# Two bottleneck blocks with batch normalization: normalizing the first group of a slot inside the first convolution, a shorter mean in the last statistics, and idle matmuls in three pauses

## The chip, the cores and the metric

The kernel runs on one core of a Trainium2 chip. Five engines of the core work side by side, each in its own order: TensorE (PE in the profile; PEld is its loading of weights), VectorE (DVE), ScalarE (ACT), GpSimd (POOL) and SyncE (SP), which here only issues transfers. Engines wait for each other by semaphores. The metric is the device time of one execution in microseconds. Before the change the median of three runs is 1983.51 us (1981.97 to 1983.78).

## The reference

The input x has 64 images of 1024 channels and 14 x 14 pixels, in fp32. Two blocks follow each other. Each is:

```python
out = relu(_bn(_conv(x, w1, b1, 1, 0), g1, be1))    # 1x1, 1024 -> 256 channels
out = relu(_bn(_conv(out, w2, b2, 1, 1), g2, be2))  # 3x3, 256 -> 256 channels
out = _bn(_conv(out, w3, b3, 1, 0), g3, be3)        # 1x1, 256 -> 1024 channels
out = softplus(residual_scale)[0] * out
return relu(x + out)
```

`_bn` subtracts the mean over all images and pixels of a channel and multiplies by the inverse root of the variance, so no value of a convolution can be normalized before all of that convolution has been computed. That is where the borders between stages come from.

## The kernel before

**Layout.** Channels lie on the 128 partitions. The 256 middle channels are two *slots* (MS = 2) of 128, and `y_all` holds them for all 12544 pixels. The pixels are cut in 32 tiles of two images (T = 32, 392 pixels), or, for the second convolution, in eight groups (NG) of eight images (1568 pixels).

**First convolution.** `Conv1` computes one unit (a pair of tiles in block 0, one tile in block 1) by seven matrix products `p1` to `p7` in place of eight (a Strassen form, class `Seven`). `stream` runs the units behind each other; the last two products of a unit, `p4` and then `p3`, are issued within the next unit, or at the end for the last one. `p4` gives the result of slot 1, which ACT evicts; `p3` gives a part of slot 0, which DVE evicts with `scalar_tensor_tensor` (L371). After each result `bn_stats` collects its statistics (L374). In block 1 this stage runs together with the last convolution of block 0 (`fused`).

**Second convolution.** `conv2` is a 3x3 convolution in a form with transformed filters (loaded by SP as tiles `ua` and `ub`) and transformed rows. It begins with four matmuls of the identity into the `columns` banks (L553). The first group of pixels has to be normalized first: `first_norm(s)` computes scale and shift of a slot (`affine_of`), then ACT normalizes the lower rows of the group (L529) and DVE the upper six (`norm_vector`, L535 and L537). `combine` then makes the inputs of the products for slot 1 and after it for slot 0: `steps` (L576; two rows are scaled by ACT, L573), `r` (L665), `sums` (L607), `v` (L613) and `diffs` (L623). PE multiplies `sums`, `v` and `diffs` by the filters, into `columns`, `m` and `l`; results come out as `f` (L780, L782). Each later group is normalized by ACT while the one before it is computed.

**Gram.** The statistics of the last convolution are not taken from its output. `gram` normalizes y again with the second convolution's statistics (`norm_to`: L529 on ACT, L974 on DVE), transposes it in pieces `zt` (the first seven by PE, L1004, and copied by DVE, L1010; the others by transfers into the buffers `homes` and DVE's transpose, L1016), and multiplies each piece with itself into the banks `cp` and `ap`.

**Last statistics.** `conv3_stats` makes mean and variance of the 1024 output channels from these: `g0` and `g1` are the sums divided by the number of pixels, with the mean of each slot in their last column (`means`). Six products `t0`, `t1` of g with the weights w3 follow, DVE multiplies them by w3 again (`q`, L1085 and L1086), and one-column matmuls into the bank `ax` sum over partitions: 16 for the mean (8 output slots, 2 input slots each; L1089), 8 for the second moment (L1091). Before them PE computes the first two of eight products of the first tile (`made`, L1353), which stay in PSUM until scale and shift are known. `residual` then finishes the first tile, and `fused` (block 0) or `final` (block 1) the others.

**What sets the order.** A scheduler orders the instructions of each engine by priorities; `tc.keep_in_program_order` holds an instruction to the place where the program issues it. PE's matmuls, many of DVE's and ACT's steps at the borders are held so. Each engine takes its instructions strictly in its order, so one that waits holds back those behind it.

Of the kernel before, what the change touches and what calls it, by code (L numbers as in the profile page):

```python
# [37 lines left out]
FP = mybir.dt.float32  # L38
# [49 lines left out]
def bottlenecks(ctx: ExitStack, tc: tile.TileContext, x, w1s, w2s, w3s, pars, out):  # L88
# [77 lines left out]
    def matmul(*args, **kw):  # L166

        tc.keep_in_program_order(nc.tensor.matmul(*args, **kw))  # L168

    def filters(pieces, spare):  # L170


# [149 lines left out]
    class Conv1(Seven):  # L322
# [2 lines left out]

        prefix = "a"

        def __init__(self, psum, pool, xs, ts, w1, par, stats):
            self.psum, self.pool, self.ts, self.par, self.stats = psum, pool, ts, par, stats
            self.a, self.s = w1  # L330
            self.n = n = len(xs) * PX // 2
            px = [slice(0, n)] * 2 if len(xs) == 2 else [slice(0, n), slice(n, 2 * n)]
            self.b = [
                [xt[:, h * CS // 2 : (h + 1) * CS // 2, p] for xt, p in zip((xs[0], xs[-1]), px)] for h in range(2)
            ]
# [15 lines left out]
        def last(self):  # L351

            yield from self.p4()
            yield from self.p3()

        def end(self):
# [3 lines left out]
        def result(self, o, i, bank, more=None):  # L360
            bias = self.par[:, B1 + o : B1 + o + 1]
            if len(self.ts) == 2:
                y = whole = two(self.ts[i], o)
            else:
                whole = two(self.ts[0], o)
                y = whole[:, i * H // 2 : (i + 1) * H // 2]
            ps, more = (v and v.rearrange("p (h l) -> p h l", l=G * W) for v in (bank, more))
            if more is None:
                act(y, ps, AF.Identity, bias=bias)
            else:  # L370
                nc.vector.scalar_tensor_tensor(y, ps, bias, more, ALU.add, ALU.add)  # L371
            if len(self.ts) == 2 or o != i:

                nc.vector.bn_stats(self.stats[:, o, self.ts[i % len(self.ts)], :], whole)  # L374

        def after1(self):
            self.u1 = self.saved("au1")
# [161 lines left out]
    def conv2(psum, pool, b, par, aff, affine_of, stats):  # L539
# [101 lines left out]
        def combine(g, pair, before=None):  # L641
# [10 lines left out]
            if pair[0] == 1:  # L652
# [3 lines left out]
                for part in slots:  # L656
                    if before is not None:
                        before(part.start)
                    last(t1[:, :, RT - 1], g, 2, -3.0, part)
                    last(t2[:, :, RT - 1], g, 1, -3.0, part)  # L660
                    for s in range(part.start, part.stop):
                        two_rows = y_all[:, s, g * GPX : g * GPX + 4 * full * LINE]
                        two_rows = two_rows.rearrange("p (r h l) -> p r h l", r=full, h=2)
                        run(stt(t[:, s, :full], two_rows[:, :, 0], -4.0, two_rows[:, :, 1]))
                    run(nc.vector.tensor_add(ra[:, part], t1[:, part], t2[:, part]))  # L665
                    if before is not None:
                        for make in x.add_columns, x.step_columns, x.subtract_columns:
                            make(slice(0, 1), part)
                nc.vector.tensor_sub(rb, t1, t2)
                if before is None:  # L670
                    x.add_columns()
                else:
# [228 lines left out]

        def first_norm(s):

            affine_of(s)
            top = 6
            norm(s, y_grp[:, s, 0, top:], aff)
            norm_vector(s, y_grp[:, s, 0, :top], aff)

        def items():
            for g, pair in pairs:  # L910
# [22 lines left out]
        for k in range(NG * NF):  # L933
            item, more = queue[0], queue[1:2]
            qs = (EVEN, ODD)
            if item.first:
                item.columns(*qs)
                qs = ()
            item.middle()
            if qs and more:  # L940
                item.columns(qs[0])
                qs = qs[1:]
            for v in more:
                v.start()
            long_work(*divmod(k, NF))
            item.columns(*qs)
            finished.send(item)
            queue = queue[1:] + list(itertools.islice(made, 1))

    def conv3(psum, t, o, w3, tag=None):  # L950
        ps = psum.tile(tag=tag)
# [106 lines left out]
                beside[k]()  # L1058
        return g0, g1

    def conv3_stats(psum, one, grams, w3, mv, tags):


        g0p, g1p = grams
# [7 lines left out]
        quad = psum.tile(2 * CS, "ax").rearrange("p (o k) -> p o k", k=2)  # L1072
        ones = one.tile([P, 1], FP, tag="ones", name="ones")
        nc.vector.memset(ones, 1.0)
        half = CS // 2
        q = one.tile([P, MS, C], FP, tag="q", name="q")
        for h in range(2):
# [7 lines left out]
                nc.vector.tensor_mul(qs[s], t, w3[:, s, cols, :].rearrange("p o c -> p (o c)"))  # L1085
            nc.vector.tensor_add(qs[0], qs[0], qs[1])  # L1086
        for o in range(CS):
            for s in range(MS):
                matmul(quad[:, o, 0:1], w3[:, s, o, :], means[s], start=(s == 0), stop=(s == MS - 1))  # L1089
        for o in range(CS):  # L1090
            matmul(quad[:, o, 1:2], q[:, 0, o * P : (o + 1) * P], ones, start=True, stop=True)  # L1091
        nc.vector.tensor_copy(mv, quad)
# [46 lines left out]
            unit.go_out()  # L1139
        residual(psum, xs[T - 1], 1, T - 1, a, aff)  # L1140

    def fused(psum, pool, xpool, xs, w1, w3, aff, par, stats):

# [9 lines left out]

        def first_convs():
            for t in range(T):
                yield Conv1(psum, pool, xs[t : t + 1], (t,), w1, par, stats)

        a, c = stream(first_convs()), stream(last_convs())  # L1160
        for i in range(LAG):
# [35 lines left out]
    def affine(mv, par, g, be, conv_bias=None, to=None):  # L1197
# [39 lines left out]
                )  # L1237
        return scale, shift

    def softplus(par):  # L1240

        a = par[:, RS : RS + 1]
# [30 lines left out]
    with tc.tile_pool(name="first", bufs=1) as one, tc.tile_pool(  # L1273
# [5 lines left out]
        for b in range(2):  # L1279
            p = keep.tile([P, NPAR], FP, tag=f"par{b}", name=f"par{b}")  # L1280
            nc.scalar.dma_start(out=p, in_=pars[b][:, :NPAR])
            par.append(p)
        sps = [softplus(p) for p in par]
        masks.make_identity(nc, ident)
        w1 = combine_w1(w1, sums_tile(one, 1)[:, 0])

        for t, xt in enumerate(pair):
            plain_conv1(psum, t, xt, w1[0], par[0], stats1)

# [11 lines left out]
        def items():  # L1301
            for t in range(2, T, 2):
                xs = [load_x(xpool, 0, t + i) for i in range(2)]
                yield Conv1(psum, one, xs, (t, t + 1), w1, par[0], stats1)

        for _ in stream(items(), beside):
            pass
# [1 line left out]
    for b in range(2):  # L1309
        pb = par[b]  # L1310
        minus_c = keep.tile([P, MS], FP, tag="minus_c", name="minus_c")
        nc.vector.tensor_scalar(minus_c, pb[:, BE2 : BE2 + MS], 0.0, -1.0, ALU.max, ALU.mult)
        aff = [small.tile([P, MS], FP, tag=f"by_slot_{n}", name=n) for n in ("scale", "shift")]

        def affine_of(s):
            mv = aggregate(stats1[:, s : s + 1], T - 3 + b)
            affine(mv, pb, G1 + s, BE1 + s, to=[v[:, s : s + 1] for v in aff])

        stats2 = keep.tile([P, MS, 1 + PARTS, nc.vector.BN_STATS_DIM], FP, tag="stats2", name=f"stats2_{b}")
        with tc.tile_pool(name=f"conv2_{b}", bufs=1) as pool, ExitStack() as scope:  # L1320
            conv2(Psum(scope, ["l"], l=2, m=2), pool, b, pb, aff, affine_of, stats2)

        with tc.tile_pool(name=f"last_{b}", bufs=1) as one, tc.tile_pool(
            name=f"last_x_{b}", bufs=4 if b == 0 else 5
# [5 lines left out]
            with ExitStack() as scope:  # L1330
# [4 lines left out]
                with tc.tile_pool(name=f"gram_{b}", bufs=1) as pool:  # L1335
# [14 lines left out]
                    beside = {FIRST + STEPS * RUN // (CH * 32): combined}  # L1350
                    grams = gram(psum, pool, homes, aff, minus_c, beside)

                    made = [conv3(psum, 0, o, w3, "cx" if b else "ay") for o in range(2)]  # L1353
                    mv3 = small.tile([P, CS, nc.vector.BN_AGGR_DIM], FP, tag="mv3", name="mv3")
                    conv3_stats(psum, pool, grams, w3, mv3, ("cy", "cp", "cy", "cp" if b else "cx"))
                if b == 1:
                    made += [conv3(psum, 0, o, w3, tag) for o, tag in zip(range(2, 6), ("cy", "cp") * 2)]
                aff = affine(mv3, pb, G3, BE3, conv_bias=B3)
# [4 lines left out]
                with tc.tile_pool(name=f"rest_{b}", bufs=1) as pool:  # L1363
                    if b == 1:
                        final(psum, pool, xpool, xs, w3, *weights, aff)
                        return
                    stats1 = stats_tile(MS, f"stats1_{b + 1}")
                    fused(psum, pool, xpool, xs, *weights, aff, par[b + 1], stats1)


# [38 lines left out]
```

## Time and profile before

The profiled execution took 1982.28 us as timed; its span in the trace is 1980.2 us, at a mean granted TensorE clock of 0.991.

| Stage, us from the start of the span | length | PE busy | DVE busy | ACT busy | share of the transfers |
|---|---|---|---|---|---|
| start of the second convolution, block 0: 300 to 320 | 20 | 14.62 | 15.65 | 7.06 | 0.49 |
| its first group: 320 to 360 | 40 | 37.30 | 38.12 | 19.97 | 0.53 |
| its other groups: 360 to 592 | 232 | 230.07 | 226.38 | 171.56 | 0.65 |
| border to the gram: 592 to 600 | 8 | 2.05 | 7.19 | 3.19 | 0.53 |
| gram: 600 to 671 | 71 | 69.92 | 50.86 | 23.21 | 0.87 |
| last statistics and first tile: 671 to 697 | 26 | 24.82 | 13.57 | 5.57 | 0.03 |
| last and next first convolution together: 697 to 1265 | 568 | 566.66 | 399.74 | 311.66 | 0.43 |
| start of the second convolution, block 1: 1285 to 1300 | 15 | 9.74 | 13.93 | 5.15 | 0.64 |
| last convolution of block 1: 1678 to 1980 | 302 | 293.59 | 263.20 | 171.00 | 0.89 |

Each row is a stretch of the trace with the busy time of the engines in it. A stage in which PE is busy for nearly all of its length can only become shorter if PE has less to do or works faster; one in which PE has gaps is set by what PE waits for. The profile also shows how an idle gap ended: `[3.15 <-DVE sums L607]` behind an instruction says that its engine was idle for 3.15 us before it, until DVE's `sums` at line 607 was done. `issue` there means that the profile shows nothing that the engine waited for.

A matmul of fp32 shows as two records, so `x8` with 128x392 are four matmuls.

### The profile page before, as it was taken

How to read it: one execution, taken by the hardware profiler on the slowest of the kernel's cores; microseconds unless marked ns; L12 is line 12 of the kernel's file. 1: busy time of each engine (PE TensorE's matmuls, PEld its weight loads, DVE VectorE, ACT ScalarE, POOL GpSimd, SP SyncE). 2: the span in 40 equal slices, each digit the busy share in tenths (PEclk: the TensorE clock that was granted, in tenths of full speed). 3: DMA queues.
4: the chain of work that ended last, by engine and by line, in shares of the span. 5: the costliest groups of instructions: out<-in, count | busy, mean ns of one | idle time of the engine just before them, and what ended most of it. 6: DMA issues, size and time to landing. Idle time of an engine off the chain costs nothing.

```text
span 1980.2 us, 27057 instructions
## 1 busy us (share of the span) xinstructions
PE 1926.9 (97%) x9432; PEld 1619.1 (82%) x9432; DVE 1582.8 (80%) x2554; ACT 1017.1 (51%) x2039; POOL 540.6 (27%) x638
## 2 busy tenths in 40 slices
PE   8999998999998999999999999989999899999998
PEld 5555557999997789999999999979999887555555
DVE  5778758999997566776776776699999974888997
ACT  1222214677765055555555555447777631555555
POOL 0111100000105133433433433201010060666665
PEclk9999999999999999999999999999999999999999
DMA  7776724676748534444444444257676385799998
GB/s 291 272 255 241 256 98 154 182 209 194 201 138 211 186 131 171 186 165 171 185 165 171 184 167 171 90 183 203 201 192 203 117 209 210 248 330 333 342 335 298
DMA packets 188983, 408.39 MB, mean 206 GB/s; under 512 B 24944, under 2 KB 165136, under 8 KB 172336
## 3 DMA queue, kind: packets, MB, share of 16 engines
q1 hardware_dynamic: 161728, 324.66, 47.8%
q0 software_dynamic: 21504, 30.94, 6.7%
q10 hardware_dynamic: 5616, 51.06, 6.1%
q8 instruction: 75, 1.23, 0.2%
q14 instruction: 60, 0.49, 0.1%
HBM read 263.75 MB, written 115.34 MB: 191 GB/s over the span
## 4 chain that ended last, share of the span: by engine, by line
PE 84%; DVE 10%; DMA 3%; issue 1%; ACT 1%; POOL 0%; DVEq 0%; SPq 0%; ACTq 0%
PE ay L168 17%; PE cy L168 14%; PE columns L168 11%; PE cp L168 11%; PE ap L168 10%; PE m L168 5%; PE l L168 5%; PE ax L168 5%; PE cx L168 4%; DMA x<-mid 2%; DVE x L446 2%; DMA out<-x 1%; PE ps L168 1%; DVE x L504 1%; DVE f L782 1%
## 5 line engine op out<-in xcount | busy, mean ns | idle before, releaser
L320 ACT ACTIVATE cu<-cy,scale 128x196 f32<-128x196 f32 (+1 forms) x552 | 256.9, 474 | 298.7 <-PE cy L168 291.4
L168 PE MATMUL columns<-v,ub 128*128 128x224 f32 (+1 forms) x1536 | 302.1, 338 | 0.7 <-ACT columns L741 0.7
L168 PEld LDWEIGHTS columns<-v,ub 128*128 128x128 f32 x1536 | 270.4, 189 | 4.4 <-ACT columns L741 1.2
L320 ACT ACTIVATE x<-x,shift 128x392 f32<-128x392 f32 x368 | 211.6, 614 | 68.5 <-POOL x L472 52.8
L446 DVE SCALAR_TENSOR_TENSOR x<-cp,scale,x 128x196 f32<-128x196 f32 (+1 forms) x368 | 178.1, 484 | 84.2 <-PE cp L168 81.3
L168 PE MATMUL cy<-ct,ws 128*128 128x196 f32 (+1 forms) x736 | 221.7, 383 | 2.5 <-ACT cu L320 2.5
L467 POOL TENSOR_TENSOR x<-x,cu 128x196 f32<-128x196 f32 (+1 forms) x184 | 167.7, 912 | 170.8 <-ACT cu L320 170.4
L168 PE MATMUL ay<-at,ws 128*128 128x196 f32 (+1 forms) x752 | 209.3, 381 | 1.0 <-ACT au L320 1.0
L472 POOL TENSOR_TENSOR x<-x,cu 128x392 f32<-128x392 f32 x124 | 125.9, 1015 | 190.7 <-DVE x L446 185.9
L168 PEld LDWEIGHTS ay<-at,ws 128*128 128x128 f32 x752 | 136.3, 190 | 35.1 <-ACT au L320 1.9
L168 PEld LDWEIGHTS cy<-ct,ws 128*128 128x128 f32 x736 | 133.6, 190 | 37.0 <-ACT cu L320 4.1
L168 PE MATMUL l<-diffs,ub 128*128 128x224 f32 (+1 forms) x768 | 149.6, 338 | 5.6 <-issue 3.2
L168 PE MATMUL m<-sums,ua 128*128 128x224 f32 (+1 forms) x752 | 145.9, 337 | 3.1 <-DVE sums L607 3.1
L493 POOL TENSOR_TENSOR x<-x,cu 128x392 f32<-128x392 f32 x120 | 125.0, 1042 | 84.1 <-DVE x L446 75.1
L852 POOL DMA_DIRECT2D y<-f x24 | 31.1, 1533 | 411.7 <-DVE f L782 411.7
L168 PEld LDWEIGHTS l<-diffs,ub 128*128 128x128 f32 x768 | 133.7, 189 | 9.6 <-PE columns L168 5.0
L168 PEld LDWEIGHTS m<-sums,ua 128*128 128x128 f32 x752 | 131.3, 189 | 4.9 <-DVE sums L607 4.5
L320 ACT ACTIVATE au<-ay 128x196 f32<-128x196 f32 (+1 forms) x141 | 53.6, 380 | 158.2 <-PE ay L168 157.6
L446 DVE SCALAR_TENSOR_TENSOR x<-cx,scale,x 128x196 f32<-128x196 f32 (+1 forms) x184 | 89.2, 485 | 52.0 <-PE cx L168 51.8
L168 PE MATMUL cy<-y,w 128*128 128x196 f32 (+1 forms) x404 | 126.8, 400 | 0.0
L168 PE MATMUL cx<-y,w 128*128 128x196 f32 (+1 forms) x404 | 125.3, 396 | 0.0
L168 PE MATMUL cp<-zt 128*128 128x257 f32 x392 | 120.1, 388 | 1.7 <-DVE zt L1010 1.7
(203 smaller groups left out, 3990.4 us busy)
## 6 DMA issues: line engine op xcount, KB each, us to landing
x<-in_x SPq DMA_DIRECT2D x62, 1568.0 KB, 6.9
ub<-u SPq DMA_DIRECT2D x94, 768.0 KB, 5.3
x<-mid SPq DMA_DIRECT2D x32, 1568.0 KB, 10.3
mid<-x ACTq DMA_DIRECT2D x31, 1568.0 KB, 5.1
out<-x SPq DMA_DIRECT2D x123, 392.0 KB, 6.9
ua<-u SPq DMA_DIRECT2D x94, 256.0 KB, 3.0
u<-y POOLq DMA_DIRECT2D x48, 256.0 KB, 6.0
home<-y SPq DMA_DIRECT2D x90, 96.0 KB, 4.0
```

What stands on the lines that cost most here:

```text
L168: tc.keep_in_program_order(nc.tensor.matmul(*args, **kw))
L320: tc.keep_in_program_order(nc.scalar.activation(*args, **kw))
L446: nc.vector.scalar_tensor_tensor(v, bank, self.scale[:, o : o + 1], v, ALU.mult, ALU.add)
L467: nc.gpsimd.tensor_add(self.part(1, 1), self.part(1, 1), u3)
L472: nc.gpsimd.tensor_add(v, v, self.u12)
L493: nc.gpsimd.tensor_add(v, v, self.u12[:, i * self.n : (i + 1) * self.n])
L504: nc.vector.tensor_scalar(v, v, self.shift[:, o : o + 1], 0.0, ALU.add, ALU.max)
L782: nc.vector.tensor_add(to, v, ls)
L852: nc.gpsimd.dma_start(out=out_rows[0][:, o], in_=f[:, o], accum_op=ALU.add)
```

## The change

There are six edits.

1. **Slot 1 normalized in the last unit of the first convolution.** In the last unit, between `p4` and `p3`, `one_done` computes scale and shift of slot 1 and lets ACT normalize its first group. DVE's eviction of `p3` and the statistics behind it are held to their place after that (`run`). `first_norm(0)` does the same for slot 0 at the start of the second convolution. ACT normalizes whole slots now; DVE's part (`norm_vector`) is gone at this place.
2. **`combine` for the first tile kind.** The two scaled rows of a last tile are made by one activation instead of two. In the first group `subtract_columns` runs once for both slots, after both, and `rb` is held to its place.
3. **Table of the square root early.** An activation `root`, whose result nobody reads, asks for the square root after the softplus, so that ACT's function table is loaded there and not before the first `sd`.
4. **Idle matmuls.** `busy` issues matmuls of the identity with a 448-wide broadcast column, whose results nobody reads: two at the start, before the first product, and six at the end of each second convolution.
5. **Mean in the last statistics.** Two activations on ACT scale w3 by the means of the two slots, into a free `homes` buffer, and POOL adds them (`by_mean`). Eight one-column matmuls with ones replace sixteen.
6. **One product less ahead.** Of the first tile's products only the first is computed before the statistics, the second right after.

```diff
+    def busy(psum, tag, n):
+        for i in range(n):
+            matmul(psum.tile(448, tag), ident, ident[:, :1].to_broadcast([P, 448]), start=True, stop=True)
...
         def last(self):
             yield from self.p4()
+            if self.one_done is not None:
+                self.one_done()
             yield from self.p3()
...
-                nc.vector.scalar_tensor_tensor(y, ps, bias, more, ALU.add, ALU.add)
+                self.run(nc.vector.scalar_tensor_tensor(y, ps, bias, more, ALU.add, ALU.add), o, i)
...
+        def run(self, ins, o, i):
+            if self.one_done is not None and (o, i) == (0, 1):
+                tc.keep_in_program_order(ins)
...
-                    last(t1[:, :, RT - 1], g, 2, -3.0, part)
-                    last(t2[:, :, RT - 1], g, 1, -3.0, part)
+                    end = y_all[:, part, (g + 1) * GPX - 2 * LINE : (g + 1) * GPX]
+                    nc.scalar.activation(t[:, part, RT - 1], end, AF.Copy, scale=-3.0)
...
-                        for make in x.add_columns, x.step_columns, x.subtract_columns:
+                        for make in x.add_columns, x.step_columns:
                             make(slice(0, 1), part)
-                nc.vector.tensor_sub(rb, t1, t2)
+                if before is not None:
+                    x.subtract_columns(slice(0, 1))
+                run(nc.vector.tensor_sub(rb, t1, t2))
...
         def first_norm(s):
-            affine_of(s)
-            top = 6
-            norm(s, y_grp[:, s, 0, top:], aff)
-            norm_vector(s, y_grp[:, s, 0, :top], aff)
+            if s:
+                affine_of(0)
+            else:
+                norm(s, y_grp[:, s, 0], aff)
...
             queue = queue[1:] + list(itertools.islice(made, 1))
+        busy(psum, "m", 6)
...
+        by_mean, more = (spare[:, s * C : (s + 1) * C] for s in range(MS))
+        for s, to in enumerate((by_mean, more)):
+            nc.scalar.activation(to, w3[:, s].rearrange("p o c -> p (o c)"), AF.Identity, scale=means[s])
+        nc.gpsimd.tensor_add(by_mean, by_mean, more)
...
         for o in range(CS):
-            for s in range(MS):
-                matmul(quad[:, o, 0:1], w3[:, s, o, :], means[s], start=(s == 0), stop=(s == MS - 1))
+            matmul(quad[:, o, 0:1], by_mean[:, o * P : (o + 1) * P], ones, start=True, stop=True)
...
+    def first_affine(b, stats):
+        aff = [small.tile([P, MS], FP, tag=f"by_slot_{n}", name=n) for n in ("scale", "shift")]
+        def affine_of(s):
+            mv = aggregate(stats[:, s : s + 1], T - 3 + b)
+            affine(mv, par[b], G1 + s, BE1 + s, to=[v[:, s : s + 1] for v in aff])
+        def one_done():
+            affine_of(1)
+            norm(1, y_grp[:, 1, 0], aff)
+        return aff, affine_of, one_done
...
         sps = [softplus(p) for p in par]
+        nc.scalar.activation(small.tile([P, 1], FP, tag="root", name="root"), sps[1], AF.Sqrt)
         masks.make_identity(nc, ident)
+        busy(psum, "ay", 2)
...
-                    made = [conv3(psum, 0, o, w3, "cx" if b else "ay") for o in range(2)]
+                    made = [conv3(psum, 0, 0, w3, "cx" if b else "ay")]
...
-                    conv3_stats(psum, pool, grams, w3, mv3, ("cy", "cp", "cy", "cp" if b else "cx"))
+                    conv3_stats(psum, pool, grams, w3, mv3, ("cy", "cp", "cy", "cp" if b else "cx"), homes[1])
+                made.append(conv3(psum, 0, 1, w3, "cx" if b else "ay"))
```

## The prediction

> **What bounds the kernel now.** I read the totals first, then TensorE's waits, then the timeline at the stage borders. TensorE (PE) is busy for all but 53 us of the 1980.2 us span:
>
> ```profile
> PE 1926.9 (97%) x9432; PEld 1619.1 (82%) x9432; DVE 1582.8 (80%) x2554; ACT 1017.1 (51%) x2039; POOL 540.6 (27%) x638
> PE 84%; DVE 10%; DMA 3%; issue 1%; ACT 1%; POOL 0%; DVEq 0%; SPq 0%; ACTq 0%
> PE cy L1004 <- issue: 11.5, 2, 5.7
> PE columns L168 <- DVE sums L607: 6.2, 2, 3.2
> ```
>
> The waits (total, times, longest) sit at borders, once per block: before the gram (L1004) and at the start of the second convolution. Within stages PE is full, so what a border saves should reach the end. The start of the second convolution in block 0:
>
> ```profile
> 307.62 1.14 ACT L529 ACTIVATE y<-y,shift,scale 128x896 f32<-128x896 f32 x1 [2.41 <-DVE shift L1234]
> 308.91 0.86 DVE L576 SCALAR_TENSOR_TENSOR steps<-y 128x672 f32<-128x672 f32 x1
> 311.02 1.75 PE L168 MATMUL columns<-sums,ua 128*128 128x224 f32 x8 [1.33 <-issue]
> 317.46 2.75 PE L168 MATMUL columns<-sums,ua 128*128 128x224 f32 x8 [3.15 <-DVE sums L607]
> 324.57 0.45 DVE L780 SCALAR_TENSOR_TENSOR f<-columns,par,ls 128x224 f32<-128x224 f32 x1 [1.59 <-ACT ls L749]
> 355.87 1.75 PE L168 MATMUL l<-diffs,ub 128*128 128x224 f32 x8 [1.61 <-issue]
> ```
>
> PE starts slot 1 at 311.02 and slot 0 only at 317.46, because slot 0's statistics and norm queue on VectorE (DVE) behind slot 1's work. From 324.57 DVE runs without a gap until PE's last wait here, at 355.87 for `diffs`. DVE sets the pace until then, PE afterwards. In the last statistics:
>
> ```profile
> 673.55 1.02 PE L168 MATMUL cy<-w,g 128*128 128x512 f32 x2
> 678.70 3.63 PE L168 MATMUL ax<-g,w 128*128 128x1 f32 x32
> 682.19 2.52 PE L168 MATMUL ax<-ones,q 128*128 128x1 f32 x16
> 684.58 2.96 PE L168 MATMUL cx<-y,w 128*128 128x392 f32 x4
> 687.33 2.82 PE L168 MATMUL cy<-y,w 128*128 128x392 f32 x4
> 4.60 22.75 PE L168 MATMUL ps<-x,w 128*128 128x392 f32 x64 [4.60 <-DMA w<-in_w]
> ```
>
> Every fp32 matmul is two records. A 392-wide record takes 0.33 us elsewhere (x8 in 2.63 in the chain), but 0.65 from 684.58 to 689.9: half speed after one-column matmuls. The last line is the kernel's head: 64 x 0.3294 = 21.1 us, so 1.7 us of slow records.
>
> [...] the trace has 1.28 at 303.63. [...] the trace's adds (0.60 at 196 columns, 1.015 at 392) give 2.1 ns.
>
> **Head.** Two idle matmuls (4 records of 448 columns: 448/392 x 0.653 = 0.75 us slow, 3.0 together) need only `ident`, done at 1.32, and end near 4.4, before the weights' 4.60. They can recover between 0 ([...] x parts bind: PE waited 0.48 for one at 5.58) and 1.7: I take 0.8. The square-root table load moves to ScalarE (ACT) at about 12.1: 1.28 + 0.2 ends near 13.6, before the first eviction at 14.22, so it costs nothing.
>
> **Second convolution, block 0.** Removed: the load at 303.63 (`sd` could start at 304.55, not 304.92: 0.37), and DVE's norm passes, 2 x (0.63 + 0.51). Added: ACT norms whole slots (1.69 each). Step by step:
> - `sd` 304.55, reciprocal 304.87, `shift` of slot 1 after 1.0 (as 312.20 to 313.20 in slot 0's chain): 305.87. No eviction stands between any more.
> - ACT norm of slot 1: 305.92 to 307.61. Meanwhile DVE evicts slot 0 from 305.81 (PE done 305.65), statistics, aggregate: 307.35. `sd` of slot 0 queues behind the norm: 307.55; `shift` 308.87.
> - ACT norm of slot 0: 308.92 to 310.6. DVE `steps` of slot 1 at 308.82, `sums` end 2.0 later: PE starts 310.9 (was 311.02).
> - DVE `steps` of slot 0 at 308.82 + 2.40 = 311.22, `sums` end 313.2. PE, through with slot 1 at 313.9, goes on without a pause[...]: `l` at 316.95 (was 322.29).
> - DVE reaches the 128x2688 subtraction 8.35 after 308.82, at 317.17, ends 320.1; `f` follows at once: 320.06 against 324.57. **4.5 us**, kept to 355.87 because DVE's order holds the same work up to `diffs`.
> SP's filter loads wait for the slot-0 eviction (L371), now 0.6 later; they land in 2.2 us (ua) and 3.8 (ub) at best, 7.1 and 8.5 at worst. The first ones are unlikely to pass PE's need at 310.9 and 312.4.
>
> **Block 1.** No table load; aggregate 1285.42 gives `shift` of slot 1 at 1287.0 (was 1287.5), norm to 1288.75, which now holds `sd` of slot 0 (1288.7); `shift` 1290.0, `steps` of slot 1 1289.97 (later than 1288.92), PE starts 1292.05 (was 1291.14), `f` at 1301.2 against 1304.57: **3.4 us**. SP's loads start 1.5 later; PE's start is later too.
> Together 7.9; bounds 5 (a late filter) and 9.6.
>
> Two activations of a last tile become one in every group: ACT has room there (171.6 of 232 us), so nothing.
>
> **Gram border.** Six idle matmuls (12 records x 0.373 = 4.5 us) run from 592.65 to 597.1, inside the 5.75 us wait that ends at 598.40. They delay nothing. Slow records cost 1.06 against 0.60 until 604, but DVE's queue absorbs much: zt's first copy stays at 599.55, the third can move 0.9 only. From 597.1 to 600.3 there are only transposes[...]. I take 0.5 per block, **1.0**; bounds 0 and 2.4.
>
> **Last statistics.** One first-tile product moves behind: 1.32 us earlier for all that follows, `cy<-w,g` at 672.23, one-column matmuls from 677.4 (DVE's `q` ends 680.3 - 1.3 = 679.0). Mean matmuls: 16 records instead of 32, 1.8 us, end 679.2. `by_mean` must be ready by 677.4: ACT from 671.45, two of 128x1024 (between 1.13 at 896 and 1.65 at 1536: 1.24, less overlap) to 673.9; POOL add 0.2 + 1024 x 2.1 ns = 2.35: 676.3. PE waits for nothing. `q` matmuls end 681.0 to 681.3 (were 684.7). Then PE has three products (12 records) until the fifth, at 689.95 before. If the clock stays up: 3.9 us to 684.9, held to 685.3 by the first eviction: 4.6 gained. If it falls for 4 us as before: 6.1 slow and 5.9 fast records, 687.2: 2.7 gained. Block 1 likewise: 1662.3 + 8.6 = 1670.9 or 1668.2 against 1673.20: 2.3 or 5.0. One-column work shrinks from 5.8 and 6.6 us to 3.6[...]. I take the middle, **3.6 each, 7.2**. In block 1 the fifth `x` load needs the `home` buffer, now until 1660 and not 1641; the pair wants it near 1692 and a load lands in 10.3.
>
> **Sum** 0.8 + 7.9 + 1.0 + 7.2 = 16.9 us of the profiled 1980.2 span (1982.28 as timed; the others 1981.97 to 1983.78). Taken off the median 1983.51: 1966.6, I say 1967.
>
> **Rivals.** (1) The clock doesn't do what idle matmuls are for: head 0, gram 0, statistics 2.7 + 2.3; 7.9 + 5.0 = 12.9, 1970.6. [...] (2) At the border only DVE's removed work counts (2.28 + 0.15 for merged `diffs`, 2.4 a block), new waits on ACT eating the rest: 0.8 + 4.8 + 1.0 + 7.2 = 13.8, 1969.7. For it: DVE sets the pace there; against: 1.59 us of DVE idle at 324.57 also goes. (3) The last stage takes it back: transfers fill 0.89 of it and PE idles 8.4 of 302 us. Against: its loads wait for outputs, which move with compute. About 1983. (4) Slower: `by_mean` goes through POOL, and PE's queue stands behind it. It costs from 3.4 us of add on (673.95 to 677.4); beyond 12 us in both blocks it outweighs everything: at 14, 2 x 10.6 - 16.9 gives 1988. Against: POOL's rate, even its 1175 ns rows, gives 2.8.
>
> **How the numbers follow.** Mine 0.46, (1) 0.28, (2) 0.14, (3) 0.06, (4) 0.06. Mine alone spans 1960.2 (all upper bounds, 23.3) to 1970; with (1), (2) and a late filter (10 us in all) 1975. Faster by over 0.2% (4 us, about what tells from no change) 0.88, same 0.06, slower 0.06.
>
> **What would show it.** Second slot's `columns<-sums` following the first without a gap; `l` 5 us earlier relative to the last eviction; x16 `ax<-ones,home` at 0.11 us without a POOL wait; the products after them at 0.33 or 0.65; cp<-zt records before 604 at 0.30 or 0.53. A wait of PE on POOL, or new DVE waits on ACT between 309 and 356, would make it wrong.

## The result and the profile after

The changed kernel takes 1970.07 us (median of four runs, 1964.93 to 1972.92) against 1983.64 us for the kernel before (1981.97 to 1984.72): ratio 0.9929, interval 0.9906 to 0.9953. That is 13.6 us or 0.7% less. The forecast was 1967 in a range of 1960 to 1975. Run twice more, beside other kernels, the changed kernel took 1966.11 and 1966.89, which is 15.6 and 14.6 less than the runs of before beside it.

Totals and waits of TensorE, changed kernel (a wait line is total, times, longest):

```profile
PE 1932.2 (98%) x9428; PEld 1617.8 (82%) x9428; DVE 1578.6 (80%) x2544; ACT 1022.2 (52%) x2026; POOL 545.0 (28%) x640
PE m L168 <- DVE sums L619: 6.2, 4, 2.6
PE cy L1019 <- issue: 2.4, 2, 1.2
```

PE is busier than before (1932.2 for 1926.9), since the idle matmuls count as busy (3.35 us at the head, 4.69 before each gram). What fell is its idle time, from 53 to 39 us. The waits of `columns` for `sums` are gone and the one before the gram fell from 11.5 to 2.4, but a wait of `m` for `sums` has grown; it comes back below. The start of the second convolution in block 0, all engines:

```profile
306.07 1.69 ACT L541 ACTIVATE y<-y,shift,scale 128x1568 f32<-128x1568 f32 x1 [1.07 <-DVE shift L1252]
308.90 0.85 DVE L588 SCALAR_TENSOR_TENSOR steps<-y 128x672 f32<-128x672 f32 x1
311.01 1.75 PE L168 MATMUL columns<-sums,ua 128*128 128x224 f32 x8 [1.03 <-issue]
314.13 1.67 PE L168 MATMUL columns<-sums,ua 128*128 128x224 f32 x8
320.16 0.44 DVE L794 SCALAR_TENSOR_TENSOR f<-columns,par,ls 128x224 f32<-128x224 f32 x1
347.64 2.52 PE L168 MATMUL m<-sums,ua 128*128 128x224 f32 x8 [2.61 <-DVE sums L619]
349.96 2.66 PE L168 MATMUL columns<-v,ub 128*128 128x224 f32 x8
352.46 1.68 PE L168 MATMUL l<-diffs,ub 128*128 128x224 f32 x8
```

Slot 0 follows slot 1 without a pause, at 314.13 and not 317.46. `f` is 4.4 us earlier than before. But of that lead only 3.4 arrive at the `l` of 352.46 (355.87 before): `m` waits 2.61 us where it waited 1.08 before, and then it and the `columns` behind it take 2.5 and 2.7 us in place of 1.7. TensorE's clock has fallen: the trace has it granted at half speed from 348.53 to 351.94. The last statistics of block 0, TensorE and POOL:

```profile
668.72 1.02 PE L168 MATMUL cy<-w,g 128*128 128x512 f32 x2
670.56 2.35 POOL L1093 TENSOR_TENSOR home<-home 128x1024 f32<-128x1024 f32 x1 [20.88 <-ACT home L1092]
673.87 1.84 PE L168 MATMUL ax<-ones,home 128*128 128x1 f32 x16
675.57 2.98 PE L168 MATMUL ax<-ones,q 128*128 128x1 f32 x16
678.41 2.96 PE L168 MATMUL ay<-y,w 128*128 128x392 f32 x4
681.16 2.41 PE L168 MATMUL cx<-y,w 128*128 128x392 f32 x4
```

POOL's add takes 2.35 us and ends at 672.9, before PE comes to the mean matmuls at 673.87, so PE doesn't wait for it. The 16 mean records take 1.84 us; the 16 of `q`, the same in number and shape, take 2.98, and the product after them 2.96 in place of 1.48. The clock falls while `q` is summed (granted half speed from 676.21 to 683.04).

**Where the time came from, in three executions.** I measured the lead over the trace of before at the border of each stage: the end of the last product of the first convolution, of the second convolution and of the gram, the first product on `ct` after the first tile, and the end of the span. Each row is what the lead grew by in that stage, in us; the columns are three traces of the same changed kernel.

| stage | forecast | first | second | third |
|---|---|---|---|---|
| head and first convolution | 0.8 | -0.2 | -0.3 | -0.6 |
| second convolution, block 0 | 4.5 | 3.3 | 3.3 | 3.4 |
| gram, block 0 | 0.5 | 0.4 | 0.6 | 0.5 |
| last statistics and first tile, block 0 | 3.6 (2.7 or 4.6) | 1.8 | 1.8 | 3.5 |
| both convolutions together | 0 | 0.0 | 0.0 | 0.0 |
| second convolution, block 1 | 3.4 | 2.4 | 3.8 | 3.8 |
| gram, block 1 | 0.5 | 0.7 | 0.8 | 0.5 |
| last statistics and first tile, block 1 | 3.6 (2.3 or 5.0) | 1.8 | 3.4 | 3.4 |
| last stage | 0 | -1.2 | 1.0 | -1.3 |
| sum | 16.9 | 9.0 | 14.4 | 13.2 |

These executions took 1972.92, 1967.56 and 1968.74 us. So the first trace shows the slowest of the changed kernel's four runs above, and a reader of it alone would put the gain at 9.0. Four stages differ by 1.4 to 2.2 us between executions of one program: in three of them TensorE ran at half speed for longer in the worse case, and in the last stage its waits for DVE's `x`, which waits for loads, differ (3.9, 1.3 and 3.6 us in the three traces, 2.8 before).

### The profile page after: what moved, and what is told of

It is laid out like the page before. It is cut to its first block, busy times and chain, and to the rows that moved or that the text cites. A ratio compares the mean times of both kernels' runs of the same rounds, so it can differ in the third digit from the quotient of the medians.

```text
span 1971.1 us, 27055 instructions
## 1 busy us (share of the span) xinstructions
PE 1932.2 (98%) x9428; PEld 1617.8 (82%) x9428; DVE 1578.6 (80%) x2544; ACT 1022.2 (52%) x2026; POOL 545.0 (28%) x640
## 4 chain that ended last, share of the span: by engine, by line
PE 85%; DVE 7%; DMA 5%; issue 1%; ACT 1%; SPq 0%; POOL 0%; DVEq 0%; ACTq 0%
PE ay L168 17%; PE cy L168 13%; PE columns L168 13%; PE cp L168 11%; PE ap L168 10%; PE m L168 6%; PE l L168 6%; PE ax L168 5%; PE cx L168 4%; DMA x<-mid 3%; DVE x L458 1%; DMA out<-x 1%; PE ps L168 1%; DVE x L516 1%; DMA home<-y 1%
```

## The experiments

The theory to test: each part of the change is worth what its border shows, and what is missing from 16.9 us lies where the clock falls. Its rivals: the gain lies in the clock alone; the order at the border does nothing; the clock's falls are hidden behind DVE. Every kernel was timed in turn with the kernel before.

### The border alone

The changed kernel with the old last statistics and without idle matmuls:

```diff
-        busy(psum, "m", 6)
-        busy(psum, "ay", 2)
-        by_mean, more = ...
-            matmul(quad[:, o, 0:1], by_mean[:, o * P : (o + 1) * P], ones, ...)
+            for s in range(MS):
+                matmul(quad[:, o, 0:1], w3[:, s, o, :], means[s], ...)
+                made = [conv3(psum, 0, o, w3, "cx" if b else "ay") for o in range(2)]
```

> The changed kernel without its idle matmuls and with the old last statistics (32 mean matmuls, two products ahead of them), so only the order at the second convolution's start is left of the change. Theory A (each part is worth what the two traces show at its place): 3.6 us in block 0 and 2.4 in block 1, so 6 us less than before, about 1977.5, with the first f near 320 and PE waiting some 2.6 us for sums near 347, as in the changed kernel. Theory B (the border is worth the 7.9 us forecast and the trace of the changed kernel caught an unlucky clock): about 1975.5, with 4.5 us of lead at the l after that wait. Theory C (the gain lies in the clock and not in the border): 1981 or more.

1976.27 us against 1981.74: ratio 0.9974 (0.9965 to 0.9984), so 5.2 us (3.2 to 6.9). In time that is near theory A's 6 and below B's 7.9; C is out. TensorE at the wait for `sums`, in this kernel's trace:

```profile
348.85 1.78 PE L168 MATMUL m<-sums,ua 128*128 128x224 f32 x8 [2.61 <-DVE sums L619]
350.47 1.69 PE L168 MATMUL columns<-v,ub 128*128 128x224 f32 x8
352.64 1.75 PE L168 MATMUL l<-diffs,ub 128*128 128x224 f32 x8 [0.48 <-PE columns L168]
```

The wait is the same 2.61 us, but here the clock did not fall. The first convolution of this execution ended 1.4 us later than before's (307.0 for 305.6), so the lead at `l`, 3.2, is 4.6 from that end: the forecast's 4.5 against the trace of before. The step holds where the clock does. In block 1 the stage gains 3.5 in this trace, so the two together have B's size; what brings them down to 5.2 comes up under the second convolution below.

### The last statistics alone

```diff
-            for s in range(MS):
-                matmul(quad[:, o, 0:1], w3[:, s, o, :], means[s], ...)
+            matmul(quad[:, o, 0:1], by_mean[:, o * P : (o + 1) * P], ones, ...)
-                    made = [conv3(psum, 0, o, w3, ...) for o in range(2)]
+                    made = [conv3(psum, 0, 0, w3, ...)]
+                made.append(conv3(psum, 0, 1, w3, ...))
```

> The kernel before with only the last statistics changed: 16 mean matmuls from by_mean, and one product moved behind them. Theory A: 1.8 us a block as in the changed kernel's trace, 3.5 in all, about 1980. Theory B (the middle of the forecast): 7.2, about 1976.4. Theory C: the clock doesn't fall in this schedule and 9.6 come, 1974. If 128x1 matmuls count as idle for the clock, the products after them run at 0.65 us a record for some 4 us in both blocks, and A is right.

1971.27 us against 1981.74: 0.9948 (0.9936 to 0.9961), 10.3 us less (7.7 to 12.7): more than A's 3.5 and B's 7.2 and nearest to C's 9.6, but C's reason, a clock that doesn't fall, holds in one block only. The trace has both cases in one execution. TensorE after the mean in block 0, then in block 1:

```profile
678.03 1.93 PE L168 MATMUL ax<-ones,q 128*128 128x1 f32 x16
679.82 1.56 PE L168 MATMUL ay<-y,w 128*128 128x392 f32 x4
...
1653.52 2.85 PE L168 MATMUL ax<-ones,q 128*128 128x1 f32 x16
1656.24 2.96 PE L168 MATMUL cx<-y,w 128*128 128x392 f32 x4
```

In block 0 nothing is slow and the stage gains 4.8 us on before, close to the forecast's 4.6 for a clock that stays up. In block 1 the clock falls in `q`, and it gains 1.8. The two make 6.6 us. The rest of this execution's 9.7 lies in stages that the edit does not touch: 1.8 in the last stage, small amounts with either sign, and 1.7 at the start of the second convolution of block 0. There both kernels run the same code with the same wait, but in the trace of before the records after it were slow and here they are not. TensorE in this kernel:

```profile
318.17 1.78 PE L168 MATMUL columns<-sums,ua 128*128 128x224 f32 x8 [3.16 <-DVE sums L607]
```

So the trace of before, too, is one draw: its 2.75 us at this place were part of what the forecast counted as to be gained. What the edit doesn't explain of the 10.3 was not followed further.

### Without idle matmuls

```diff
-        busy(psum, "m", 6)
-        busy(psum, "ay", 2)
```

> The changed kernel without both groups of idle matmuls (two at the head, six ahead of each gram). Theory A: the head gave nothing (x parts bind), the two gram borders 0.1 and 0.9: 1 us slower than the changed kernel run beside it. Theory B: the idle matmuls are worth what the forecast said, 1.8 us. Rival: they are worth 4 or more, because the place where the clock recovers spreads further (then the spread of 8 us among the changed kernel's runs goes with them, and this one's runs lie within 3 us like before's).

1967.55 us, and the changed kernel beside it 1966.11 (next section): 1.4 us slower, with intervals that overlap (0.9915 to 0.9940 and 0.9908 to 0.9935). The time fits the forecast's 1.8 and theory A's 1, but can't tell them from nothing; the rival's 4 or more is out. The heads of the two kernels, TensorE, first this kernel and then the changed one:

```profile
4.79 24.21 PE L168 MATMUL ps<-x,w 128*128 128x392 f32 x64 [4.79 <-DMA w<-in_w]
```

```profile
1.37 3.35 PE L168 MATMUL ay<-ident 128*128 128x448 f32 x4 [1.37 <-POOL ident masks.py:199]
4.52 23.02 PE L168 MATMUL ps<-x,w 128*128 128x392 f32 x64
```

Here the head's 64 records take 24.2 us, 23.0 with idle matmuls in front of them. The end of the first convolution, in all traces of this study: 305.6, 306.3, 307.0 and 307.3 us in the four kernels without idle matmuls at the head, 305.4 to 306.2 in the ten with them. The mean differs by 0.85 us, though the two groups overlap. The trace of before happened to be the best of the four, which is why the table shows a loss at the head. At the gram's borders this kernel gains 0.6 and 0.3 without idle matmuls, as against 0.4 to 0.8 with them: these few cases show no benefit. All traces together do (see the gram below).

### The changed kernel once more

No edit; a second trace beside its variants.

> The changed kernel once more, unaltered, for a second trace and more times beside its variants: about 1970, between 1963 and 1974. If the spread is the clock's, the mean granted clock goes with the time (0.002 of 1970 us at half speed is 4 us), and the two traces differ at the places where a wait of 1 to 3 us or one-column matmuls let it fall: the m after the wait for sums, the cp of the gram, the products of the last statistics. If it is the transfers', they differ in the last stage, by waits for x<-mid.

1966.11 us against 1981.74: 0.9922 (0.9908 to 0.9935). The second column of the table is its trace. Clock and time go together as expected: 0.994 in the executions of 1972.92 and 1971.74 us, 0.996 in those of 1968.40 and 1964.93, 0.995 in this one of 1967.56. The first two traces differ where the clock fell in one of them (block 1's `m`: 2.07 and then 3.12 for `columns` in the first, 1.78 in the second; block 1's `q`: 2.44 against 1.93) and in the last stage, by a transfer. Both halves of the expectation hold. The last stage of the first trace has this wait, TensorE, then DVE:

```profile
1883.81 0.93 PE L168 MATMUL cp<-y,ws 128*128 128x392 f32 x2 [1.24 <-DVE x L458]
1883.13 0.62 DVE L458 SCALAR_TENSOR_TENSOR x<-cp,scale,x 128x392 f32<-128x392 f32 x1 [1.00 <-DMA x<-mid]
```

### Both products ahead again

```diff
-                    made = [conv3(psum, 0, 0, w3, ...)]
+                    made = [conv3(psum, 0, o, w3, ...) for o in range(2)]
-                made.append(conv3(psum, 0, 1, w3, ...))
```

> The changed kernel with both first products ahead of the statistics again, the mean matmuls still 16 from by_mean: this takes the moved product apart from the halved mean matmuls. Theory A (the forecast's step: everything after starts 1.32 us earlier where the product is moved): 1.3 us a block slower than the changed kernel, 2.6 in all, near 1969. Theory B: the product only changes places, and what it saves ahead it costs behind at half speed: 0 to 1 us. Theory C: with 1.32 us of full work more ahead, the clock's fall hits elsewhere, and the time goes either way by 3.

1966.35 us against 1982.75: 0.9925 (0.9910 to 0.9941), no slower than the changed kernel. That is theory B's side, but the six runs lie between 1964.30 and 1974.60, so the time alone doesn't exclude A's 2.6. The traces say more. Where the clock falls (block 1) this kernel's stage gains 1.75 us, like the changed kernel's 1.75 in its first trace: the 1.32 us saved ahead of the statistics are paid behind them at half speed. Where it stays up (block 0) it gains 3.2, since PE then runs out of products and waits 1.68 us for a bank; the kernel with only the last statistics changed, its product moved, gained 4.8. So the moved product is worth its price only with the clock up; this rests on one case each. The slow end, 1974.60, is the traced run: one wait of 2.90 us for DVE's `x` in its last stage let the clock fall for 6.8 us, and the stage lost 3.9.

### The wait for sums filled

```diff
+            if k == NF - 1:
+                busy(psum, "m", 6)
             for v in more:
                 v.start()
```

> The changed kernel with six idle matmuls (12 records of 0.19 us, 2.2 us) put into the 2.61 us wait of m for sums, once per block. Theory A: that wait lets the clock fall in some executions (m 2.5 and the columns after it 2.7 or 3.1 us in place of 1.7), which costs 1.0 us in block 0 and up to 1.0 in block 1; filled, it doesn't fall: 1 to 2 us less than the changed kernel, 1964 to 1965, and both places show 1.7. Rival: the time there is DVE's (diffs ends only at 351.3 in the first trace), so a slow m is hidden: no difference.

1965.38 us against 1982.75: 0.9913 (0.9900 to 0.9926), about what theory A says. TensorE there:

```profile
344.74 4.69 PE L168 MATMUL m<-ident 128*128 128x448 f32 x12
349.27 1.67 PE L168 MATMUL m<-sums,ua 128*128 128x224 f32 x8
350.78 1.69 PE L168 MATMUL columns<-v,ub 128*128 128x224 f32 x8
```

Nothing is slow here any more (1.67 and 1.69 us for the records behind the filling), and the second convolution of block 0 gains 4.2 us for 3.3. The rival (hidden behind DVE) is out. The expectation had the price of a record wrong, though: 12 records take 4.69 us and not 2.2, so the filling is 2 us longer than the wait and `m` itself starts at 349.27 and not at 347.64. By that price three idle matmuls (6 records, some 2.3 us) would fill most of the wait: an estimate from this trace, which was not run.

### The product between the one-column matmuls

```diff
         for o in range(CS):
             matmul(quad[:, o, 0:1], by_mean[...], ones, ...)
+        product()    # the second product of the first tile
         for o in range(CS):
             matmul(quad[:, o, 1:2], q[...], ones, ...)
```

> The changed kernel with the second first-tile product put between the two groups of 16 one-column matmuls and not after them. Theory A (one-column work counts as idle for the clock, and 3.6 us of it in one piece let it fall): in two pieces of 1.8 with 1.3 of full work between, the clock stays up; mv is ready at the same time or up to 1.3 later, the products after it take 0.33 us a record: 1.5 us less in block 0 and up to 3 in block 1 against the changed kernel, 1962 to 1964. Rival: [...] the clock falls anyway and mv comes 1.3 later: 1 to 2 us slower.

1965.15 us against 1982.75: 0.9914 (0.9901 to 0.9926). TensorE in block 0:

```profile
673.43 1.84 PE L168 MATMUL ax<-ones,home 128*128 128x1 f32 x16
675.13 1.56 PE L168 MATMUL ay<-y,w 128*128 128x392 f32 x4
676.53 1.84 PE L168 MATMUL ax<-ones,q 128*128 128x1 f32 x16
678.24 1.56 PE L168 MATMUL cx<-y,w 128*128 128x392 f32 x4
...
682.81 1.56 PE L168 MATMUL ay<-y,w 128*128 128x392 f32 x4 [1.69 <-DVE x L1124]
```

The clock stays up: the same 32 one-column records and the same product, in another order. The stage gains 3.2 us in block 0, where PE runs out of products and waits 1.69 us for a bank, and 5.1 in block 1, the forecast's 5.0. Over all traces: with the one-column matmuls in one piece of 3.6 us the products after them were slow in 13 of 16 cases (eight traces, two blocks each), in two pieces of 1.8 us in none of 8. Theory A.

### Both, and nine idle matmuls

The two edits above together, on the changed kernel:

> Both of the above. Theory A: the sum of the two, 3 to 5 us less than the changed kernel, about 1962, and a spread smaller than its 8 us, since no place is left where the clock falls by luck but the gram borders. Rival: as the better of the two, or as the changed kernel.

> The kernel with the product between the one-column matmuls and the filled wait, once more beside the changed kernel on one chip: 1962 to 1964, 3 us less than the changed kernel, and clock 0.999 to 1.000. If the 3 us seen were the chip's, both come out alike.

1963.13 us against 1982.75 (0.9903, 0.9889 to 0.9917), and again 1963.85 against 1981.44 (0.9910, 0.9896 to 0.9923). It is faster than both kernels: its eight times lie between 1962.30 and 1964.23, the changed kernel's fourteen between 1964.76 and 1973.06. The spread has shrunk from 8 to 2 us, and the granted clock of the traces is 1.000 and 0.999. Of the expected 3 to 5 us about 3 came. The changed kernel in the second of these comparisons:

> The changed kernel once more, for the comparison with its improved variants on one chip: 1966, between 1964 and 1973; clock 0.994 to 0.996.

1966.89 us (1964.76 to 1973.06); 0.9931 (0.9917 to 0.9944). With nine idle matmuls ahead of each gram in place of six:

```diff
-        busy(psum, "m", 6)
+        busy(psum, "m", 9)
```

> The changed kernel with the product between the one-column matmuls, the filled wait for sums, and nine idle matmuls ahead of each gram in place of six (they end about when the first transpose starts). Theory A: the clock falls in the gram's first records only in some executions, and nine push the last idle record 1.1 us nearer to them: up to 1 us less than with six, 1962 to 1963. Rival: the transposes start late because of the norm, and three more idle matmuls delay the second block's by up to 0.3: same as with six.

1964.57 us (0.9911, 0.9897 to 0.9925): the rival. The gram's first records are at full speed in both blocks, and 18 idle records last 6.96 us and hold the first transpose back by about a microsecond. The gram's stages gain 0.8 and 0.7 all the same, as with six in the first trace of the kernel above (0.7 and 0.7); what this trace has less than that one lies in its last stage.

### The norm late again

```diff
-            if self.one_done is not None:
-                self.one_done()
             yield from self.p3()
...
-            if s:
-                affine_of(0)
-            else:
-                norm(s, y_grp[:, s, 0], aff)
+            affine_of(s)
+            norm(s, y_grp[:, s, 0], aff)
```

> The changed kernel with slot 1's aggregate, affine and norm back at the head of the second convolution, so that slot 0's statistics queue on DVE behind slot 1's combining again; norms still on ACT, tile ends still in one activation. Theory A (the order is what saves at the border): slot 0's shift comes after slot 1's combining, near 313.5, its ACT norm ends near 315.2, and the first l starts near 321, as in the kernel before: 4 us slower per block than the changed kernel, 7 to 8 in all, near 1974. Theory B (only DVE's removed norm work and merged diffs count, the second rival of the forecast): no slower than the changed kernel by more than 2 us.

1971.54 us against 1981.44 (0.9948, 0.9936 to 0.9961), and 1966.89 for the changed kernel beside it: 4.7 us slower, with intervals that just overlap. Theory B, the forecast's second rival, allowed 2; theory A asked for 7 to 8. The time lies between the two. TensorE's start on slot 0 in block 1 of this kernel:

```profile
1289.29 2.57 PE L168 MATMUL columns<-sums,ua 128*128 128x224 f32 x8 [2.29 <-DVE sums L617]
```

The pause is back, and the clock falls behind it. In block 1 nearly the whole lead goes with the order: the first `l` is 0.3 us ahead of before, counted from the end of the first convolution, and 4.0 in the changed kernel. In block 0 the late order keeps 3.7 of 5.3. Of these, 1.7 are the clock: it held in this trace (1.78 and 1.70 us for the records after the wait) and had fallen in that of before (2.75 and 2.44). For the rest, the table load (1.28 us at 303.63 in the trace of before) is gone from before the first `sd`, the held evictions let slot 1's `shift` end at 305.8 and not 307.6, and DVE has no norm passes; these parts do not need the new order. How they divide the remaining 2.0 among them was not taken apart.

## Why the prediction was right, and where its terms were off

**Direction and size** were right: 13.6 to 15.6 us for a forecast of 16.5, and the parts measured alone (5.2, 10.3 and 1.4 for the idle matmuls, 16.9 together) add up to a little more than the whole. That 16.9 is also the forecast's sum is chance: of the 10.3 the trace shows only 6.6 in the stages that were changed.

**Head**, forecast 0.8: a mean of 0.85 over the traces, four against ten. The trace of before, at the lucky end, hides it. The 0.48 us at 5.58 that the forecast calls a wait of PE is one of its weight loading; the matmuls ran on.

**Second convolution.** Step by step as forecast in block 0: shift of slot 1 ends at 306.04 (305.87), norm of slot 0 starts at 309.02 (308.92), slot 0 without a pause, `f` at 320.16 (320.06). In block 1 PE started 1.0 us later, counted from the end of the first convolution (0.9), and the lead at `l` grew by 3.4 where the clock held. No filter came late. The step that failed is "kept to 355.87 because DVE's order holds the same work": DVE keeps its lead (`diffs` starts at 350.25 and not 354.68), but PE doesn't. The scheduler put `r` of the second group behind the first group's statistics (at 344.40; before, ahead of them at 343.94, although all else was some 5 us later there), so `sums` behind it comes only 3.3 us earlier (346.50 for 349.83). PE, now ahead, waits 2.61 us in place of 1.08, and in 10 of 16 cases (eight traces, two blocks) its clock fell at that wait. Against the traces where it held (4.6 and 3.4), the fall costs 1.3 us in block 0 and 1.0 in block 1. And both sums were reckoned from a trace of before that had fallen in the same way at 317.46 (worth 1.7 us) and at 1297.45 (3.11 and 2.09 us for the records, 1.7 too much). In an execution of before without these falls less is left to gain: 4.6 and 3.5 in the trace of the border alone, less 1.7 each, are 4.7 by this estimate, which fits its 5.2 us.

**The window.** In all fourteen traces every half-speed stretch within the kernel lasts 3.41 us or a multiple of it, and within a trace they start whole multiples of 3.413 us apart (in the changed kernel's first trace at 348.53, 597.70, 676.21, 1324.74 and 1652.42: 73, 96, 286 and 382 times 3.413 after the first). So I cut each trace at these edges into windows. TensorE in the windows around the wait for `sums` in block 0, the changed kernel's first trace and then the border alone (stretch, length, busy time and records, granted clock, then the transfers' share and GB/s):

```profile
345.11:348.53 3.42, 0.89 (x5) 1.00 0.30 110
348.53:351.94 3.41, 3.41 (x11) 0.50 0.08 24
344.67:348.08 3.41, 1.56 (x9) 1.00 0.64 227
348.08:351.49 3.41, 2.64 (x14) 1.00 0.00 0
```

The wait is 2.61 us in both. In the first it lies almost whole in one window, which leaves 0.89 us of work there; in the second the edge of a window divides it. I counted every full-speed window of the fourteen traces, taking no one-column matmul as work and leaving out windows with transposes: all 40 that had at most 1.42 us of work were followed by half speed, and none that had 1.47 or more. In the trace of before, the window from 591.18 to 594.59 had 1.47 us and the clock held; the one from 314.70 to 318.11 had 0.65 us, all of it behind the 3.15 us wait for `sums`, and half speed starts at 318.11. The count accounts for all 16 waits and for all cases of one-column matmuls, in one piece and in two. So what differs between these executions is where the window's edge falls.

**Gram**, forecast 0.5 each: 0.4 to 0.8 measured, but the kernel without idle matmuls shows 0.6 and 0.3. What they do to the clock is plain: in the four traces without them 6.83 us of half speed lie around the start of each gram (8 of 8 cases), in the ten with them 3.41 us in 8 of 20 cases and none in 12. In time it shows only in the mean: the stage gains 0.61 us over these 20 cases and 0.23 over the 6 of the three other kernels without them, so 0.4 a block. That the transposes behind the idle matmuls lose some of it was the author's estimate. In the kernel with both products ahead PE had 1.92 us of work from 594.45 to 597.87, 1.28 of it transposes, and the clock held, where the 0.64 us of other work alone would be far below the 1.42 above; in the changed kernel's first trace it fell after 1.74 us, 1.28 of it transposes (594.29 to 597.70). How much of a transpose counts was not taken apart.

**Last statistics**, forecast 3.6 each out of 2.7 or 4.6, and 2.3 or 5.0. POOL's add (2.35 us) and the mean records (1.84) were exact to 0.05, and full speed gives 4.8 (statistics alone) and 5.1 (product between), as forecast. The term that was off is the fallen case, which the forecast gave one value. It depends on where the clock falls. Where it falls within `q`, which the forecast kept at full speed (2.44 to 2.98 us and not 1.93), the stage gains 1.8; where it falls only behind `q`, 3.4. The three traces of the changed kernel have three of each in their six cases, a mean of 2.6, and none at full speed, so the middle between full speed and fallen was too good by 1.0 per block. Moving the product, priced at 1.32 per block, bought nothing in the one pair of cases in which the clock fell behind it.

**The rivals.** The first (the clock gains nothing: 12.9 us) and the second (13.8) are at least as near to the measured 13.6 to 15.6 in their sums as the forecast, so the total doesn't tell them apart; the terms do. The first has too large a border and nothing at the head and the gram, where the idle matmuls show. The second is out in block 1 by the late norm, where nearly the whole lead went with the order; in block 0 the 2.0 us that stayed are near its 2.4. The third, a last stage that takes the gain back, is seen as a loss of 1.2 and 1.3 us in two traces and a gain of 1.0 in the third: a scatter of the transfers, not a mechanism. The fourth would have needed 12 us of POOL and met 2.35.

## What to carry to other kernels

Read a stage's price off the trace twice, with TensorE's clock up and with it down, and ask of every wait like those here (2.29 to 5.75 us) and every run of one-column matmuls like the 3.6 us here which of the two follows: what work would be left in the worst window of 3.41 us (at most 1.42 us of it was followed by half speed here)? Real work put into such a place (a product of 1.3 us between two groups of one-column matmuls) held the clock here in 8 of 8 cases; idle matmuls in the wait for `sums` held it too, but count their records at the measured time (0.39 us for 448 columns, 12 in 4.69). When a program's executions scatter by 8 us, look for the places where the clock falls in some of them only, the trace of before included, and judge a change by several traces: one trace of this change said 9 us, three say 9 to 14.

## What the runs showed of the hardware

After 3.6 us of one-column matmuls without a pause TensorE's clock fell in 13 of 16 cases; with 1.8 us of them, then 1.3 of full work, then 1.8, in none of 8. At half speed they are slow themselves: in the changed kernel's first trace the 16 of `q` took 2.98 us for 1.84, and their weight loads, one for each, 0.33 us from 676.21 on and 0.19 before. Cut on the grid of 3.413 us on which the half-speed stretches of a trace start, a full-speed window with at most 1.42 us of other matmuls was followed by half speed (40 of 40) and one with 1.47 or more was not, windows with transposes aside. So after a wait of 2.61 us the same eight records of `m` in block 0 took 1.78 us in one trace (border alone), 2.52 in another and 3.33 in a third (the changed kernel's first and third). While POOL adds two 128x1024 operands for 2.35 us, a DVE addition of 128x512 takes 1.24 us (block 0) and 1.52 (block 1) in place of 0.69, and in both it ends some 0.55 us after POOL's. Why was not shown, and it was off the path here.
